# Causal scores from high and low float32r parts in a two-layer attention block on one Trainium2 core

## The chip, the cores and the metric

The kernel runs on one core of one Trainium2 chip. The metric is the device time of one execution in microseconds, the median of three runs. Four engines matter here: PE (TensorE, matmuls, with its weight loads shown apart as PEld), DVE (VectorE), ACT (ScalarE) and POOL (GpSimd). SP issues most DMAs from one queue, in order.

## The reference

The inputs are `x` and a context `y`, 16 batches of 256 tokens by 256 features, all float32. Three attentions follow one another for every batch, each with 16 heads of 16 features, and then an MLP:

```
layer 0:  x = rmsnorm(x + softmax(q k^T / 4) v Wo)      q from rmsnorm(x), k and v from rmsnorm(y)
layer 1:  h = ln(x);  q, k, v = h W + b;  rope(q), rope(k)
          s = where(tril, q k^T / 4, -inf);  x = x + softmax(s) v Wo      (causal)
layer 2:  h = ln(x);  q = h W, k and v = y W;  rope(q), rope(k)
          x = x + softmax(q k^T / 4) v Wo
mlp:      x = x + gelu(ln(x) W1 + b1) W2 + b2            (256 -> 1024 -> 256)
```

The code numbers the layers 0, 1 and 2. The "second layer" of the change is layer 1, the only causal one.

## The kernel before, in words

There are 48 attentions, 16 batches by three layers. The string `ORDER` sets the layer of each of the 48, so that layer 1 of a batch follows some attentions after its layer 0. An `Att` object holds one attention; its methods are its steps. Most methods are generators: each `yield` ends a piece that is emitted by itself.

The order of all pieces is written out by hand in the text `PLAN`. Each word names a step (`scores.18.0` is the first block of scores of attention 18, `q.19` a piece of the queries of attention 19), and each time a word stands there the next piece of its generator is emitted. The engines run their own instructions in the order in which they were emitted, so `PLAN` sets the order on PE, DVE, ACT, POOL and SP. The last attention's end and the MLPs (eight groups of two batches) come after `PLAN`.

The steps that the text below speaks of, with their lines:

- `q` (785) and `k` (840) make queries and keys by feature: 16 matmuls through `by_feature` (631), then for layers 1 and 2 the bias on ACT (758), the rope on DVE (766 swap, 772 two products, 808 or 861 or 864 the sum). `v` and `project` are 16 matmuls each through `by_token` (643).
- Attentions that are not fast: the queries are written twice into the tile `qm`, even rows kept in one copy and odd rows in the other (DVE 814, ACT 816). One 32-row group of PE then holds two heads.
- Fast attentions: `q_high` (821) rounds the queries to float32r on ACT, into both halves of the tile; `q_low` (828, 832) takes the rest on DVE and copies it; `q_out` (838) moves rows by two DMAs so that each row pair holds high and low parts. `k_high` (873, ACT), `k_low` (877, DVE) and `k_out` (885, two DMAs) do it for the keys, through the tile `hl`, of which there is one buffer. `qm` and `kT` have two each.
- `scores` (933) makes one block of scores into two PSUM tiles `S` of two banks each, the pool's only two, then exponentiates them on ACT (974, one instruction for each tile, into `pt`), and for layer 1 clears the upper triangle on POOL (982).
- `values` (1005) multiplies with the values into `A`; `take` and `take_last` (1020) copy that out; `heads_in`, `sums_in`, `invert` and `divide` normalise, by way of DMAs.

A block of scores in both forms, where `m` is the number of query columns:

```
if not self.fast:
    for half in range(2):
        ...
        for r, ps in rows:
            nc.tensor.matmul(ps[64 * half : 64 * half + 64, 2 * m * u : 2 * m * (u + 1)] ...,
                lhsT=self.kT[r, t, at], rhs=self.qm[r, t, :, q0:S], ...)
    continue
for i in range(2):
    for h in range(2):
        for r, ps in rows:
            nc.tensor.matmul(ps[:, at : at + m],
                lhsT=self.kd[r, i, t, kc * P : (kc + 1) * P].bitcast(F32R),
                rhs=self.qd[r, i, h, t, q0:S].bitcast(F32R), start=(h == 0), stop=(h == 1), ...)
```

`rows` are four row groups. Layers 0 and 2 have four blocks of one unit each, with `m` = 256. Layer 1 has three blocks: the first and the third are one unit with `m` = 256, the second is two units with `m` = 128 (the keys of the second half, which only the second half of the queries sees). Attentions 0 and 1 are never fast.

Of the kernel before, what the change touches and what calls it, by code (L numbers as in the profile page):

```python
# [30 lines left out]
FAST = (0, 2)  # L31
# [23 lines left out]
scores.0.0 q.1 scores.0.0 scores.0.0 v.0 spread.1 scores.0.1 spread.1 q.1 v.0 v.1 v.1 scores.0.1  # L55
v.0 load_piece.5.0 scores.0.1 v.1 stats_x.2 scores.0.2 stats_x.2 stats_x.3 values.0.0 scores.0.2
values.0.1 send.2 stats_x.3 scores.0.2 load_piece.5.3 send.3 values.0.1 scores.0.3 k.1 scores.0.3
send.2 scores.0.3 load_piece.5.2 k.2 send.3 k.1
scores.1.0 k_high.2 load_early.3 k_low.2 values.0.2 scores.1.0 stats_y.2 receive.2 q.2 scores.1.0
stats_y.2 scores.1.1 load_piece.5.1 values.0.3 scores.1.1 q.3 k_out.2 take_last.0 scores.1.1 q.2  # L60
scores.1.2 q_high.2 heads_in.0 values.1.0 q_low.2 scores.1.2 load_early.4 q_low.2 v.2 v.2
scores.1.2 stats_y.3 q_out.2 scores.1.3 v.2 values.1.1 receive.3 scores.1.3 stats_x.6 load.4 k.3
scores.1.3 values.1.1
scores.2.0 k_high.3 q.3 values.1.2 stats_y.3 scores.2.0 k_low.3 values.1.3 scores.2.0 heads_in.0
load_piece.6.0 take_last.1 q_high.3 load_early.0 scores.2.1 values.2.0 q_low.3 scores.2.1 k_out.3
k.4 q_low.3 scores.2.1 sums_in.0 stats_x.4 values.2.1 stats_x.4 scores.2.2 q_out.3 load_piece.6.3
send.4 v.3 scores.2.2 v.3 send.4 load_piece.6.2 scores.2.2 invert.0 v.3 k_high.4 divide.0
scores.2.3 stats_y.6 invert.0 values.2.1 q.4 scores.2.3 k_low.4 load_piece.6.1 sums_in.1
scores.2.3 values.2.2 receive.4
scores.3.0 invert.0 values.2.3 scores.3.0 heads_in.1 fold_of_att take_last.2 scores.3.0 q.4  # L70
heads_in.1 invert.1 scores.3.1 q_high.4 divide.0 invert.1 divide.1 values.3.0 k_out.4 scores.3.1
q_low.4 project.0 stats_y.4 scores.3.1 invert.1 q_low.4 stats_y.4 fold_of_att values.3.1 project.0
q_out.4 scores.3.2 stats_x.6 project.0 scores.3.2 send.6 project.0 stats_y.8 scores.3.2 finish.0
fold_of_att values.3.1 stats.5 scores.3.3 v.4 v.4 load_later.0 scores.3.3 divide.1 stats.5
scores.3.3 k.6 load_piece.7.0 norm.5 heads_in.2 v.4 load_piece.7.1
scores.4.0 load_early.1 k_high.6 values.3.2 scores.4.0 k_low.6 values.3.3 fold_of_att fold_of_att
scores.4.0 turn.5 take_last.3 sums_in.2 stats_y.6 scores.4.1 turn.5 q.5 scores.4.1 sums_in.3
stats_x.8 load_piece.7.3 scores.4.1 fold_of_att k_out.6 k.5 invert.2 q.5 stats_x.8 invert.2
scores.4.2 q.5 k.5 divide.2 values.4.0 q.5 scores.4.2 send.6 q.5 values.4.1 scores.4.2 heads_in.2
q.5 project.1 load_later.1 k.5 invert.2 k.5 v.5 k.5 project.1 heads_in.3 values.4.1 scores.4.3 q.5  # L80
q.5 receive.6 values.4.2 k.5 heads_in.3 scores.4.3 q.6 project.1 scores.4.3 invert.3 load_early.2
project.1 divide.2 values.4.3 invert.3 q.6 v.5 load_piece.7.2
scores.5.0 take_last.4 q_high.6 finish.1 v.6 v.6 sums_in.4 scores.5.0 q_low.6 scores.5.0 q_low.6
scores.5.0 stats.7 scores.5.0 scores.5.1 invert.3 v.6 stats.7 send.8 v.5 scores.5.1 q_out.6 norm.7
project.2 scores.5.1 pieces.7 send.8 scores.5.1 stats_y.10 scores.5.2 scores.5.1 heads_in.4
values.5.0 project.2 scores.5.2 pieces.7 receive.8 project.2 values.5.1 scores.5.2 k.8 heads_in.4
divide.3 divide.3 scores.5.2 values.5.1 invert.4 scores.5.2
scores.6.0 k_high.8 divide.4 project.2 pieces_in.7 values.5.2 scores.6.0 k_low.8 load_later.7
finish.2 project.3 scores.6.0 invert.4 take_last.5 stats.9 scores.6.1 project.3 stats.9 values.6.0
sums_in.5 scores.6.1 project.3 v.7 v.7 keep.5 scores.6.1 norm.9 invert.4 load_later.8 q.7 pieces.9  # L90
invert.5 pieces.9 v.7 divide.5 scores.6.2 invert.5 q.7 load_later.9 values.6.1 scores.6.2
heads_in.5 divide.4 k.7 q.7 scores.6.2 heads_in.5 q.7 values.6.1 q.7 scores.6.3 stats_y.8
pieces_in.9 k.7 q.7 values.6.2 scores.6.3 k.7 q.8 invert.5 scores.6.3 load_later.5 k.7 k.7 k_out.8
values.6.3 k.7 project.3 q.7 q.7 take_last.6 load_later.4
scores.7.0 divide.5 sums_in.6 q.8 project.4 scores.7.0 stats_x.10 scores.7.0 stats_x.10 project.4
q_high.8 scores.7.1 heads_in.6 scores.7.0 send.10 project.4 scores.7.0 project.5 send.10
scores.7.1 stats_y.10 q_low.8 heads_in.6 scores.7.1 q_low.8 scores.7.1 v.8 project.5 stats.11
scores.7.1 q_out.8 scores.7.2 finish.3 receive.10 v.8 stats.11 values.7.0 scores.7.2 invert.6
values.7.1 norm.11 invert.6 divide.6 scores.7.2 q.9 scores.7.2 pieces.11 values.7.1 v.8 scores.7.2
scores.8.0 keep.7 pieces.11 values.7.2 scores.8.0 load_later.6 k.10 invert.6 scores.8.0  # L100
load_later.3 take_last.7 load_piece.8.1 q.9 sums_in.7 scores.8.1 load_piece.8.2 k_high.10 q.9
values.8.0 load_piece.8.0 scores.8.1 q.9 k.9 load_later.10 k_low.10 scores.8.1 divide.6 heads_in.7
q.9 scores.8.2 k.9 q.9 values.8.1 scores.8.2 k.9 v.9 v.9 scores.8.2 k.9 heads_in.7 k.9 values.8.1
scores.8.3 pieces_in.11 q.9 q.9 values.8.2 k.9 scores.8.3 k.11 invert.7 stats_x.14 k_out.10
scores.8.3 divide.7 gain_ca
scores.9.0 v.9 k.11 invert.7 k.11 values.8.3 scores.9.0 k.11 q.10 scores.9.0 take_last.8
scores.9.0 k.11 invert.7 scores.9.0 scores.9.1 q.10 project.4 k.11 sums_in.8 q_high.10 values.9.0
finish.4 project.6 scores.9.1 q_low.10 scores.9.1 q_low.10 scores.9.1 v.10 divide.7 k_high.11
q_out.10 scores.9.1 k_low.11 heads_in.8 scores.9.2 v.10 keep.9 heads_in.8 invert.8 values.9.1
scores.9.2 project.6 q.11 invert.8 project.6 scores.9.2 scores.9.2 k_out.11 v.10 values.9.1  # L110
scores.9.2
scores.10.0 stats.13 q.11 values.9.2 scores.10.0 stats.13 q.11 project.7 scores.10.0 divide.8
norm.13 load_later.2 take_last.9 q.11 scores.10.1 heads_in.9 q.11 values.10.0 scores.10.1
project.7 invert.8 k.12 load_piece.9.0 q.11 scores.10.1 sums_in.9 pieces.13 load_piece.9.1
q_high.11 scores.10.2 stats.12 values.10.1 q_low.11 pieces.13 scores.10.2 stats.12 q_low.11
scores.10.2 norm.12 q_out.11 divide.8 k.12 turn.12 invert.9 values.10.1 scores.10.3 k.12 invert.9
turn.12 values.10.2 k.12 scores.10.3 heads_in.9 k.12 v.11 v.11 divide.9 scores.10.3 load_piece.9.2
k.12 pieces_in.13 stats.16 stats_x.14 k_high.12 q.12 k_low.12 load_piece.8.3 invert.9 v.11
values.10.3 q.12
scores.11.0 take_last.10 fold_of_fc1 stats.16 q.12 scores.11.0 project.8 q.12 scores.11.0 q.12  # L120
project.6 fold_of_fc1 norm.16 scores.11.1 heads_in.10 q.12 values.11.0 scores.11.1 send.14
project.8 send.14 k.13 scores.11.1 fold_of_fc1 q_high.12 k_out.12 scores.11.2 divide.9 values.11.1
q_low.12 scores.11.2 v.12 v.12 q_low.12 scores.11.2 pieces.16 q_out.12 values.11.1 stats_y.14
scores.11.3 k.13 load_piece.9.3 v.12 pieces.16 project.9 scores.11.3 stats_y.14 k.13 scores.11.3
k.13 keep.11 k.14 project.9 heads_in.11 stats.15 sums_in.10
scores.12.0 k.13 k_high.14 stats.15 values.11.2 k.13 scores.12.0 k_low.14 scores.12.0 norm.15
pieces.15 scores.12.1 finish.6 q.13 scores.12.1 project.8 pieces.15 fold_of_fc1 scores.12.1
receive.14 values.11.3 heads_in.10 q.13 invert.10 scores.12.2 take_last.11 divide.10 scores.12.2
q.13 heads_in.11 values.12.0 q.13 scores.12.2 values.12.1 q.13 sums_in.11 q.13 scores.12.3
values.12.1 gain_fc1.0 q.13 invert.10 values.12.2 q.13 pieces_in.15 scores.12.3 fold_of_fc1 q.14  # L130
scores.12.3 invert.11 stats_x.17
scores.13.0 divide.11 keep.12 q.14 k.15 scores.13.0 stats_x.17 invert.10 q_high.14 load_piece.10.0
v.13 scores.13.0 v.13 q_low.14 invert.11 scores.13.0 k.15 q_low.14 scores.13.0 scores.13.1
# [213 lines left out]
def xattn_kernel(  # L347
# [303 lines left out]
    def fast(i):  # L651

        return 1 < i < N_ATT and ORDER[i] in FAST

# [1408 lines left out]
```

## Time and profile before

| what | value |
| --- | --- |
| median of 3 runs (lowest to highest) | 910.98 us (907.81 to 911.55) |
| the profiled execution: its time, its span | 906.3 us, 904.5 us |
| busy share of the span: PE, PEld, DVE, ACT, POOL | 97%, 63%, 77%, 63%, 39% |
| attentions: first to last exponential | 12.0 to 697.5 us |
| granted PE clock, mean | 0.997 |
| instructions of the program in the trace | 32853 |

A float32 matmul stands in the trace as two records, a float32r matmul as one. A line of the timeline gives start, duration, engine, line, operation, output and inputs, shapes and the number of records; the time from one group's start to the next group's start is what the group took of PE. Busy time of PE is not PE at its peak, since the ends of matmuls are modelled.

### The profile page before, as it was taken

The numbers are of one execution on the slowest core, as the hardware profiler recorded it, in microseconds if no ns is written. First come the engines' busy times: TensorE is split into PE (matmuls) and PEld (weight loads), VectorE is DVE, ScalarE is ACT, GpSimd is POOL, SyncE is SP. The second block draws the span as 40 slices with busy tenths as digits, with TensorE's granted clock in tenths as the row PEclk, the third lists the DMA queues.
The fourth block names the chain that finished last, engine by engine and source line by source line (L and its number), as shares of the span: only waits on it lengthen the run. The fifth ranks groups of instructions, "written<-read, shape, count | busy, mean of one in ns | idle before, by whom it ended". The sixth has DMA issues, their size and how long they took to land.

```text
span 904.5 us, 32853 instructions
## 1 busy us (share of the span) xinstructions
PE 881.5 (97%) x13762; PEld 565.6 (63%) x13762; DVE 699.5 (77%) x1534; ACT 570.8 (63%) x801; POOL 352.3 (39%) x558
## 2 busy tenths in 40 slices
PE   8989999899999999999999999999999999999997
PEld 4455545555555555554555555555555799999997
DVE  5357978888888899779887889998885687777653
ACT  3776657676777767757766677776876633334440
POOL 3334664538172546265453353573132131111000
PEclk9999999999999999999999999999999999999999
DMA  8564445535343434452434332232432021112201
GB/s 280 199 201 144 150 143 174 166 115 168 117 157 125 140 109 143 145 173 85 137 118 147 100 123 83 87 115 97 148 112 74 25 68 60 57 35 65 71 25 50
DMA packets 101454, 107.04 MB, mean 118 GB/s; under 512 B 26602, under 2 KB 81778, under 8 KB 101298
## 3 DMA queue, kind: packets, MB, share of 16 engines
q1 hardware_dynamic: 96210, 89.89, 30.1%
q0 software_dynamic: 4400, 14.42, 5.4%
q8 instruction: 110, 1.80, 0.8%
q10 hardware_dynamic: 688, 0.54, 0.2%
q14 instruction: 46, 0.38, 0.1%
HBM read 46.33 MB, written 13.65 MB: 66 GB/s over the span
## 4 chain that ended last, share of the span: by engine, by line
PE 76%; DVE 9%; DMA 5%; ACT 3%; issue 3%; SPq 3%; POOL 1%; ACTq 0%; DVEq 0%; POOLq 0%
PE d L643 14%; PE d L631 14%; PE A L1005 13%; PE S L962 7%; PE upX L1219 6%; PE A L1317 6%; PE S L951 5%; PE downZ L1317 3%; PE upZ L1219 3%; ACT pt L974 2%; PE d L1317 2%; PE d L1219 2%; DVE u L772 1%; DMA turn_hop<-bits 1%; SPq L596 1%
## 5 line engine op out<-in xcount | busy, mean ns | idle before, releaser
L974 ACT ACTIVATE pt<-S 128x1024 f32<-128x1024 f32 x224 | 217.6, 1022 | 73.1 <-PE S L951 41.6
L1005 PE MATMUL A<-pt,va 128*32 128x256 f32 (+1 forms) x3072 | 186.8, 366 | 5.1 <-DVE av L1020 2.8
L974 ACT ACTIVATE pt<-S,sy 128x1024 f32<-128x1024 f32 x128 | 135.9, 1114 | 37.3 <-PE S L962 28.3
L1005 PEld LDWEIGHTS A<-pt,va 128*32 128x32 f32 x3072 | 87.0, 109 | 81.8 <-issue 16.7
L982 POOL TENSOR_SCALAR_AFFINE_SELECT pt<-pt 128x512 f32<-128x512 f32 x128 | 93.4, 750 | 66.5 <-ACT pt L974 65.8
L962 PEld LDWEIGHTS S<-qm,kT 32*128 32x128 f32 x1920 | 68.6, 183 | 56.9 <-issue 29.7
L962 PE MATMUL S<-qm,kT 32*128 32x256 f32 x1920 | 96.4, 304 | 6.1 <-ACT pt L974 4.7
L619 POOL TENSOR_TENSOR cur<-cur,bias 128x512 f32<-128x512 f32 x48 | 65.5, 1368 | 36.5 <-DVE xn L551 36.4
L758 ACT ACTIVATE a<-d,qk_bias 128x256 f32<-128x256 f32 x128 | 53.9, 475 | 31.2 <-PE d L631 25.8
L523 POOL TENSOR_SCALAR r_ln<-bmv 128x2 f32<-128x2 f32 x48 | 14.9, 311 | 143.2 <-DVE bmv L542 142.5
L951 PE MATMUL S<-qm,kT 32*64 32x512 f32 (+1 forms) x1152 | 67.6, 512 | 1.4 <-ACT pt L974 1.2
L631 PE MATMUL d<-hT,sa 128*32 128x256 f32 x1024 | 61.6, 380 | 0.1
L1241 ACT COPY g<-upX 128x512 f32<-128x512 f32 x28 | 15.0, 589 | 72.4 <-issue 68.1
L1063 POOL TENSOR_TENSOR seen<-seen,sums 128x64 f32<-128x64 f32 x48 | 17.1, 355 | 103.9 <-DVE sums L1049 102.2
L551 DVE TENSOR_SCALAR xn<-cur,bmv,r_ln 128x256 f32<-128x256 f32 x96 | 49.9, 568 | 5.3 <-POOL r_ln L524 5.3
L772 DVE TENSOR_TENSOR u<-u,turn 128x512 f32<-128x512 f32 x64 | 53.2, 831 | 0.0
L772 DVE TENSOR_TENSOR a<-a,turn 128x512 f32<-128x512 f32 x64 | 47.5, 742 | 1.8
L1257 ACT ACTIVATE g<-g,fb 128x256 f32<-128x256 f32 x96 | 41.0, 499 | 11.1 <-DVE g L1246 11.1
L766 DVE STREAM_SHUFFLE u<-a 128x512 f32<-128x512 f32 x64 | 47.8, 747 | 0.1
L1065 DVE TENSOR_TENSOR oT<-oT,inv 128x512 f32<-128x512 f32 x48 | 34.9, 728 | 15.7 <-DMA inv<-inv_hop 5.9
L631 PEld LDWEIGHTS d<-hT,sa 128*32 128x32 f32 x1024 | 32.8, 110 | 22.6 <-ACT hT L573 0.8
L1020 DVE COPY av<-A 128x512 f32<-128x512 f32 x47 | 32.2, 685 | 13.4 <-PE A L1005 13.1
(176 smaller groups left out, 1711.4 us busy)
## 6 DMA issues: line engine op xcount, KB each, us to landing
kT<-hl SPq DMA_DIRECT2D x60, 256.0 KB
qm<-qm SPq DMA_DIRECT2D x60, 256.0 KB
oT<-av SPq DMA_DIRECT2D x192, 64.0 KB
inv<-inv_hop SPq DMA_DIRECT2D x96, 128.0 KB
turn_hop<-bits SPq DMA_DIRECT2D x33, 256.0 KB
hT<-turn_hop SPq DMA_DIRECT2D x92, 64.0 KB
out<-res SPq DMA_DIRECT2D x15, 256.0 KB
cur<-in_x POOLq DMA_DIRECT2D x11, 256.0 KB, 3.7
```

The lines of the kernel that those rows point to most:

```text
L619: nc.gpsimd.tensor_tensor(t, t, bias_sb[:, row : row + D].unsqueeze(1).to_broadcast([P, NC, D]), ALU.add)
L631: nc.tensor.matmul(o, lhsT=w[:, k, at + t * P + j : at + t * P + j + 32], rhs=tokens, start=(k == 0), stop=(k == KC - 1), skip_group_check ...
L643: nc.tensor.matmul(ps[j : j + 32, c * D : (c + 1) * D], lhsT=some_tokens(src, k, c, j), rhs=w[:, k, at : at + D], start=(k == 0), stop=(k ...
L758: nc.scalar.activation(a[:, t], ps[:, t], AF.Identity, bias=bias[:, t : t + 1])
L772: nc.vector.tensor_tensor(t, t, table.unsqueeze(1).to_broadcast([P, KC, S]), ALU.mult)
L951: nc.tensor.matmul(ps[64 * half : 64 * half + 64, 2 * m * u : 2 * m * (u + 1)] .rearrange("p (i s) -> p i s", i=2), lhsT=self.kT[r, t, at] ...
L962: nc.tensor.matmul(ps[:, at : at + m], lhsT=self.kd[r, i, t, kc * P : (kc + 1) * P].bitcast(F32R), rhs=self.qd[r, i, h, t, q0:S].bitcast(F ...
L974: nc.scalar.activation(pt[:, :, :w], ps[:, :, :w], AF.Exp, scale=scale)
L982: nc.gpsimd.affine_select(out=diag, in_=diag, compare_op=ALU.is_ge, fill=0.0, base=0, pattern=[[0, 2], [0, 2], [1, P]], channel_multiplier=-1,
L1005: nc.tensor.matmul(self.av[32 * r : 32 * r + 32, i, q0:S], lhsT=self.va[:, kc, 8 * t + 2 * r + i, :], rhs=pts[r // 2][:, r % 2, i * m : (i ...
L1219: nc.tensor.matmul(o if len(b.shape) == 2 else by_groups(o), lhsT=a[:, c * P : (c + 1) * P], rhs=b, start=(first and c % 2 == 0), stop=Tru ...
L1317: nc.tensor.matmul(ps[:, c, :], lhsT=a[f // 2][:, f % 2, c * P : (c + 1) * P], rhs=b[:, f, :], start=(first and c == 0 and f == 0), stop=True,
```

## The change

`FAST` takes layer 1 in. The scores of the 16 causal attentions are then made by the float32r branch above: 16 matmuls of 128 by 256 for each of the two wide blocks, and 32 matmuls of 128 by 128 for the block with two units. Their `q` ends before the two masked copies (lines 814 and 816 are not reached any more in these 16), their `k` writes into `hl`, and they get the steps `q_high`, `q_low` (two pieces), `q_out`, `k_high`, `k_low` and `k_out`.

`PLAN` is written anew from its first words on. It has 2720 words for 2640: each causal attention has two pieces of `q` fewer and seven pieces of the new steps more; every other word stands there as often as before. The lines below `PLAN` move down by 11 in the changed kernel (962 becomes 973). Nothing else differs.

```diff
-FAST = (0, 2)
+FAST = (0, 1, 2)
...
 PLAN = """
...
-scores.18.0 heads_in.16 q.19 k.20 scores.18.0 q.19 heads_in.16 divide.15 scores.18.0 q.19
-invert.16 k_high.20 scores.18.1 q.19 k_low.20 project.15 scores.18.1 take_last.17 stats.23
-scores.18.1 sums_in.17 divide.16 stats.23 scores.18.2 project.15 values.18.0 scores.18.2 norm.23
...
+scores.18.0 q.19 k_high.20 divide.16 load_piece.11.0 values.17.2 invert.16 scores.18.0 k_low.20
+values.17.3 q.19 scores.18.0 k_out.20 q.19 k.19 take_last.17 scores.18.1 divide.15 values.18.0
+heads_in.16 scores.18.1 q.19 project.15 scores.18.1 k.19 sums_in.17 k.19 q_high.19 scores.18.2
+k.19 receive.20 heads_in.16 values.18.1 q_low.19 scores.18.2 q_low.19 v.19 scores.18.2 k.19
+q_out.19 invert.17 k_high.19 scores.18.3 k_low.19 values.18.1 q.20 scores.18.3 stats_x.24 k_out.19
...
```

## The prediction

> **What bounds the kernel now.** I read the busy shares first, then busy time by stage, the waits, the timeline of PE, and the groups by shape. First two lines of the page, then an answer for the stretch in which only attentions run (columns: length, then busy time and instructions of PE, PEld, DVE, ACT and POOL, granted clock, DMA share and GB/s):
>
> ```profile
> PE 881.5 (97%) x13762; PEld 565.6 (63%) x13762; DVE 699.5 (77%) x1534; ACT 570.8 (63%) x801; POOL 352.3 (39%) x558
> PE 76%; DVE 9%; DMA 5%; ACT 3%; issue 3%; SPq 3%; POOL 1%; ACTq 0%; DVEq 0%; POOLq 0%
> 12.00:686.60 674.60, 660.25 (x12096) 370.05 (x12100) 553.72 (x1211) 480.13 (x611) 317.02 (x500) 1.00 0.43 138
> ```
>
> PE is busy 98% of the attention stage and holds three quarters of the chain of waits, so a microsecond less of matmul is nearly a microsecond less of time, as long as DVE (82% here) lets it. The MLPs, after 697 us, are not touched.
>
> The timeline of PE gives what a block of scores costs. Each line has the start, the duration, the engine and the line first.
>
> ```profile
> 308.91 1.93 PE L1005 MATMUL A<-pt,va 128*32 128x256 f32 x32
> 310.66 1.91 PE L631 MATMUL d<-hT,sa 128*32 128x256 f32 x32
> 312.50 0.74 PE L962 MATMUL S<-qm,kT 32*128 32x256 f32 x16
> 313.17 1.07 PE L1005 MATMUL A<-pt,va 128*32 128x256 f32 x16
> ...
> 318.49 1.11 PE L951 MATMUL S<-qm,kT 32*64 32x512 f32 x16
> 319.53 1.93 PE L643 MATMUL d<-cao,oT 128*32 128x256 f32 x32
> 321.28 1.91 PE L643 MATMUL d<-ca,yT 128*32 128x256 f32 x32
> 323.12 1.12 PE L951 MATMUL S<-qm,kT 32*64 32x256 f32 x32
> 324.17 1.93 PE L631 MATMUL d<-hT,sa 128*32 128x256 f32 x32
> ```
>
> From start to next start, the float32r block takes 313.17 - 312.50 = 0.67 us. The float32 block takes 1.04 us when it is one wide unit (318.49 to 319.53) and 1.05 when it is two narrow ones (323.12 to 324.17); I use 1.04 for both.
>
> Third, the groups on DVE and ACT that the change removes or multiplies, and two weight loads:
>
> ```profile
> L828 DVE TENSOR_TENSOR qm<-a,qm 128x512 fp32r<-128x512 f32 x16 | 13.1, 819 | 3.8 <-ACT qm L821 3.7
> L832 DVE CAST qm<-qm 128x512 fp32r<-128x512 f32 x30 | 13.5, 450 | 1.0
> L877 DVE TENSOR_TENSOR hl<-hl 128x512 fp32r<-128x512 f32 x16 | 11.6, 726 | 1.4 <-ACT hl L873 1.2
> L814 DVE TENSOR_SCALAR qm<-a,vec 128x512 f32<-128x512 f32 x16 | 7.8, 484 | 0.5
> L821 ACT CAST qm<-a 128x1024 fp32r<-128x1024 f32 x16 | 16.8, 1048 | 12.4 <-DVE a L808 7.2 <-issue 4.5 <-ACT hT L573 0.7
> L873 ACT CAST hl<-hl 128x512 fp32r<-128x512 f32 x16 | 10.0, 626 | 1.1 <-DVE hl L861 0.5 <-ACT av L1020 0.5
> L816 ACT ACTIVATE qm<-a,vec 128x512 f32<-128x512 f32 x16 | 11.6, 725 | 7.6 <-DVE a L808 6.6 <-ACT pt L974 0.9
> ...
> L962 PEld LDWEIGHTS S<-qm,kT 32*128 32x128 f32 x1920 | 68.6, 183 | 56.9 <-issue 29.7 <-ACT pt L974 19.3 <-ACT av L1020 4.3
> L1005 PEld LDWEIGHTS A<-pt,va 128*32 128x32 f32 x3072 | 87.0, 109 | 81.8 <-issue 16.7 <-POOL pt L982 13.2 <-ACT av L1020 1.8
> ```
>
> **PE, the wide blocks.** Layer 1 has two a causal attention, of a shape that layers 0 and 2 run already: 2 x (1.04 - 0.67) = 0.74 us saved.
>
> **PE, the narrow block.** 32 float32r matmuls of 128 columns against 128 weight columns have no row in the trace. The block of 0.67 us is four waves, each one matmul in each of the four row groups. A float32 record is two passes, and 16 records of `values` in four column groups take 0.89 us for 256 columns and 0.46 for 128 (medians of the timeline), so passes scale with columns; the 32 records of a dense product, 16 passes of 256 one after another in each column group, take 1.72 at the least, 0.107 a pass. Four waves are 0.43, and 0.24 is left for filling and draining. The narrow block is eight waves:
> - streaming alone, 0.053 a wave: 8 x 0.053 + 0.24 = 0.67;
> - float32 speed, four passes, 0.213 a wave: 8 x 0.213 + 0.24 = 1.95;
> - bound by weight loads: a load of 32 columns lasts 109 ns and one of 128 lasts 183, so a column costs (183 - 109) / 96 = 0.77 ns and 128 columns some 99 ns; with the wave's own overhead 0.107, hence 8 x 0.107 + 0.24 = 1.10.
>
> I take 1.10. The float32r records are single and 256 columns run at one pass, and the load's row is of the same weight shape. The ends stay for the range. So the narrow block does not gain: 1.04 becomes 1.10.
>
> The Trainium skill, TensorE: Matmul & The Clock Gate, section "LDWEIGHTS (loading the stationary operand)", states a load time of columns / 1.2 ns, which is 107 ns for 128 and agrees with the rows above; it speaks against this half of the change. The same page's "Back-to-back issue gap" has N / 2.4 + 2.5 ns for a matmul, 56 ns for 128 columns; by that rule alone the block would be an estimated 8 x 0.056 + 0.24 = 0.69 us and the whole saving 6.6 us larger.
>
> Sum on PE: 16 x (0.74 - 0.06) = **-10.9 us** (bounds: 16 x (0.74 + 0.37) = -17.8 and 16 x (0.74 - 0.91) = +2.7).
>
> **DVE.** Per causal attention: plus 0.82 (828), 0.45 (832), 0.73 (877), minus 0.48 (814), and the keys' sum into `hl` 0.77 for 0.74: +1.55, x16 = +24.7 us. Hidden only where PE has more to do. I cut `PLAN` into 47 stretches, from the first piece of `scores.i.0` to that of `scores.(i+1).0`, and added the durations of the pieces in each: 1.78 for 16 dense matmuls, 0.67 or 1.04 a block of scores, 0.87 for `values` (0.43 narrow), and DVE and ACT rows by their mean. Against the trace the totals need a factor: PE 622.6 x 1.033 = 643 (a dense group mostly takes 1.84), DVE 591.5 by words where the trace is busy 553.7 (means overlap a little; 0.925 fits the middle of the stage). With these, the larger engine of each stretch adds up to 649.6 before, and the trace took 674.5 from the first exponential of attention 0 to that of attention 47. So this sum misses 25 us of smaller waits. DVE exceeds PE by 6.4 us in all before, and by 10.9 after: worst in the stretches of attentions 18 and 37 (13.7 PE, 15.7 DVE each), 10 (12.9, 14.6), 4 and 20 (1.3 each). That is **+4.5 us** given back. Behind a late `q_low` on DVE stand `q_out` on SP and everything SP has behind it: `invert`, `k_out`, `heads_in`, whose landings `divide` and then `project` await.
>
> **ACT.** +1.05 + 0.63 - 0.73 = 0.95 a causal attention, 15 us in all, on an engine busy 71% of the stage; no stretch has ACT above PE by this. Cost nothing, hidden under PE; without that cover 15 us.
>
> **The spacing of score blocks.** The two `S` tiles come free after two exponentials (2 x 1.02, and some 0.2 to start), so less than 2.25 us of other matmuls between two blocks makes PE wait. Summed over the 176 blocks, that shortfall is 20.8 us in the old order and 14.0 in the new: layer 0 loses most of it (8.0 to 2.5). Stretch by stretch the trace's stalls go with it only in part (a correlation of 0.65), so half counts: **-3.4 us** (0 to -6.8).
>
> **New DMAs.** 64 issues more on SP, at 0.60 us (median of `k_out`'s issues) 38 us on a queue that is far from full, and 16.8 MB on engines 43% busy. They must land before `scores.i.0`. The chain shows 3.25 us for one landing of `kT` and 3.66 and 2.40 for `qm`. In the new order, PE work between `k_out` or `q_out` and the scores is at least 3.6 us in 31 of the 32 causal cases; `k_out.19` has only 1.9. I allow **+2 us** for that and for the single `hl` buffer, now used by every attention (0 to +6).
>
> **Sum:** -10.9 + 4.5 - 3.4 + 2 = -7.8 us. The profiled execution took 906.3 us (span 904.5 and 1.8 around it) and would take 898.5; the median of the runs is 4.7 above it, so 911.0 - 7.8 = **903 us**. Anything within 0.5% (4.6 us) can't be told from no change.
>
> **Rivals.**
> - *Narrow matmuls stream freely* (0.67 a block): 6.9 us more, 896. For it: 128 columns halve exactly in `values`. Against: those loads have only 32 columns.
> - *Narrow matmuls run at float32 speed* (1.95): -7.8 + 16 x 0.85 = +5.8, 917. For it: no float32r row under 256 columns. Against: the mode belongs to the operand, and 256 columns run at one pass. It decides from about 1.6 us a block.
> - *DVE becomes the bound* (the slower side): if each DVE piece holds its engine for its full mean, the larger engine of the stretches adds up to 649.4 before and 655.8 after, +6.4, with nothing back for spacing: 917. It decides, by this sum, once DVE exceeds PE by some 19 us over the stretches instead of 10.9 (10.9 + 7.8): then nothing of the gain is left. For it: 12 of the 47 stretches come out with DVE at PE's level or above. Against: before, stretches such as attention 5 (10.1 PE, 11.5 DVE) took 10.2 us, since DVE runs ahead into its neighbours.
> - *The change doesn't do what it says*, two records a matmul as in float32: excluded, since 1920 matmuls of the same form have one record each.
>
> **Chances.** Forecast 0.55, free streaming 0.15, float32 speed 0.13, DVE 0.17. Faster by over 0.5%: three quarters of the forecast and all of free streaming, 0.56. Same: 0.23. Slower: 0.21, the most part of the two slow rivals and a little of the forecast. The range 893 to 919 leaves out the tail of free streaming with full spacing gain and that of both slow rivals together.
>
> **What would show it.** Right: wide causal blocks at 0.67 from start to start, narrow ones near 1.10 with waves 0.107 apart, DVE busy some 20 us more in the stage, ACT 15 us more, no long wait of the causal scores for `kT` or `qm`. Wrong: narrow blocks over 1.6 us; PE waiting on dense products for DVE's `hT` or `oT`; PE's busy share of the stage below 95%.

## The result, and the profile after

| | before | after |
| --- | --- | --- |
| median (20 runs each) | 911.17 us | 902.21 us |
| lowest to highest | 906.73 to 916.83 | 897.72 to 909.80 |
| profiled execution, span | 906.3, 904.5 us | 904.37, 902.6 us |
| granted PE clock of the profiled execution | 0.997 | 0.989 |

The ratio is 0.9901, with a 95% interval of 0.9879 to 0.9923: about 9 us faster, where 7.8 was forecast. The profiled execution of the changed kernel is one of its longer ones, so its span is not to be set against that of before; the busy times are.

First the engines' busy shares and the chain's shares on the page of the changed kernel, then the attention stage, from the first exponential of attention 0 to that of attention 47:

```profile
PE 868.3 (96%) x13762; PEld 580.2 (64%) x13762; DVE 715.6 (79%) x1566; ACT 583.8 (65%) x817; POOL 356.7 (40%) x558
PE 60%; DVE 15%; DMA 9%; SPq 4%; issue 4%; ACT 4%; POOL 3%; ACTq 0%; DVEq 0%; POOLq 0%
...
11.50:684.30 672.80, 647.57 (x12096) 384.98 (x12100) 567.86 (x1244) 493.16 (x627) 321.58 (x501) 0.99 0.51 164
```

PE lost 13.2 us of busy time, DVE gained 16.1 and ACT 13.0. PE still fills 96% of the stage (647.57 of 672.80), but its part of the chain fell from 76% to 60% (66% in a second profile of the same kernel, `after_again` below): DVE, DMA and SP's queue took the rest. The kernel is nearer to having several bounds at once.

The blocks of scores on the timeline of PE in the changed kernel, where line 962 has become 973:

```profile
150.43 1.05 PE L1016 MATMUL A<-pt,va 128*32 128x256 f32 x16
151.41 1.11 PE L973 MATMUL S<-qm,kT 32*128 32x128 f32 x32
152.45 1.07 PE L1016 MATMUL A<-pt,va 128*32 128x256 f32 x16
...
160.75 0.75 PE L973 MATMUL S<-qm,kT 32*128 32x256 f32 x16
161.43 1.07 PE L484 MATMUL d<-fc,vec 128*32 128x256 f32 x16
```

A wide block takes 161.43 - 160.75 = 0.68 us from start to start. The narrow one, which no row of before showed, takes 152.45 - 151.41 = 1.04, against 1.05 as float32. So the whole saving in the scores' PE time comes from the 32 wide blocks.

The groups on DVE that grew, after:

```profile
L888 DVE TENSOR_TENSOR hl<-hl 128x512 fp32r<-128x512 f32 x32 | 24.1, 752 | 1.2 <-ACT hl L884 1.1
L839 DVE TENSOR_TENSOR qm<-a,qm 128x512 fp32r<-128x512 f32 x32 | 22.6, 708 | 3.4 <-ACT qm L832 3.4
L843 DVE CAST qm<-qm 128x512 fp32r<-128x512 f32 x46 | 22.2, 482 | 0.9
```

And what PE waited for (total in us, times, longest):

```profile
PE d L654 <- DVE oT L1076: 7.8, 7, 2.0
PE S L973 <- ACT pt L985: 4.2, 12, 0.6
PE S L973 <- DMA qm<-qm: 3.4, 5, 1.3
PE d L642 <- DVE va L928: 2.4, 1, 2.4
PE A L1016 <- DVE av L1031: 2.1, 2, 1.1
...
PE d L642 <- DMA hT<-turn_hop: 2.0, 3, 1.0
```

The first, the third and the last line are new: before, PE never waited for the divided heads (`oT`) or for a landing of `qm` or `hT`. They are small. The first is not the scores' doing: `order_alone`, below, has it too. The third is, but only two of its five waits stand before causal scores (attentions 9 and 13, 1.2 us together); the other three stand before attentions 14 and 37, of layers 0 and 2.

### The profile page after: what moved, and what is told of

It is laid out like the page before. It is cut to its first block, busy times and chain, and to the rows that moved or that the text cites. A ratio compares the mean times of both kernels' runs of the same rounds, so it can differ in the third digit from the quotient of the medians.

```text
span 902.6 us, 33008 instructions
## 1 busy us (share of the span) xinstructions
PE 868.3 (96%) x13762; PEld 580.2 (64%) x13762; DVE 715.6 (79%) x1566; ACT 583.8 (65%) x817; POOL 356.7 (40%) x558
## 4 chain that ended last, share of the span: by engine, by line
PE 60%; DVE 15%; DMA 9%; SPq 4%; issue 4%; ACT 4%; POOL 3%; ACTq 0%; DVEq 0%; POOLq 0%
PE d L654 11%; PE d L642 10%; PE A L1016 9%; PE S L973 7%; PE upX L1230 6%; PE A L1328 6%; DMA inv<-inv_hop 3%; PE downZ L1328 3%; PE upZ L1230 3%; ACT pt L985 3%; DMA qm<-qm 2%; PE d L1328 2%; DVE u L783 2%; PE d L1230 2%; DVE xn L562 1%
## 5 line engine op out<-in xcount | busy, mean ns | idle before, releaser
L973 PEld LDWEIGHTS S<-qm,kT 32*128 32x128 f32 x2944 | 101.2, 184 | 79.0 <-issue 45.0
L973 PE MATMUL S<-qm,kT 32*128 32x256 f32 (+1 forms) x2944 | 138.2, 300 | 8.2 <-ACT pt L985 4.2
L1016 PEld LDWEIGHTS A<-pt,va 128*32 128x32 f32 x3072 | 94.9, 111 | 63.3 <-issue 7.0
L993 POOL TENSOR_SCALAR_AFFINE_SELECT pt<-pt 128x512 f32<-128x512 f32 x128 | 96.8, 778 | 50.7 <-ACT pt L985 50.3
L1074 POOL TENSOR_TENSOR seen<-seen,sums 128x64 f32<-128x64 f32 x48 | 20.0, 417 | 109.6 <-DVE sums L1060 109.4
L1076 DVE TENSOR_TENSOR oT<-oT,inv 128x512 f32<-128x512 f32 x48 | 35.4, 737 | 18.9 <-DMA inv<-inv_hop 13.2
L1323 DVE TENSOR_TENSOR g<-g,g 128x512 f32<-128x512 f32 x64 | 40.5, 681 | 0.0
L832 ACT CAST qm<-a 128x1024 fp32r<-128x1024 f32 x32 | 33.6, 1049 | 9.8 <-issue 4.1
```

Source lines behind the costliest of these rows:

```text
L973: nc.tensor.matmul(ps[:, at : at + m], lhsT=self.kd[r, i, t, kc * P : (kc + 1) * P].bitcast(F32R), rhs=self.qd[r, i, h, t, q0:S].bitcast(F ...
L993: nc.gpsimd.affine_select(out=diag, in_=diag, compare_op=ALU.is_ge, fill=0.0, base=0, pattern=[[0, 2], [0, 2], [1, P]], channel_multiplier=-1,
L1016: nc.tensor.matmul(self.av[32 * r : 32 * r + 32, i, q0:S], lhsT=self.va[:, kc, 8 * t + 2 * r + i, :], rhs=pts[r // 2][:, r % 2, i * m : (i ...
```

## The experiments

The theory: PE gains about 0.37 us in each of 32 wide blocks, 11.8 us, and nothing in the narrow ones; some of it is given back through DVE's added work and landings, and the new order adds a little. Rivals: the gain is the new order's alone; DVE has become the bound; or the new DMAs are what gives back. The kernels ran on different chips, and each ratio is to the kernel before on the same chip. Differences between two ratios are worked out as if their errors were independent. Of the variants, only `dve_relief`, `parts_twice` and `filled_wait` stand on a chip on which the changed kernel is known to have run (`after_again`). For the others its ratio of 0.990 is carried over from chip to chip, which no run checks.

### What is the order's, and what the scores'

`order_alone`:

```diff
-FAST = (0, 1, 2)
+FAST = (0, 2)
 PLAN: k_high, k_low, k_out, q_out and the second q_low of causal attentions left out,
       their q_high and first q_low replaced by q
```

> The new order of the steps with the causal scores as they were, in float32; the steps of the high and low parts are left out, and the two masked copies of the queries come back in the places of q_high and the first q_low. Theory (the gain is PE time of the causal blocks, 0.37 us for each of 32 wide blocks and nothing for the narrow ones, 11.8 us, with some 4 given back through DVE and landings): most of the gain is gone, 907 to 913 us. Rival (the gain is the new order's spacing of the score blocks): 899 to 904 us, no slower than the changed kernel's 902.2.

Measured: 903.36 us against 906.75, ratio 0.9966 (0.9944 to 0.9987). `after_again`, the changed kernel beside two others further down:

> The changed kernel itself, unaltered, beside the other three, so that they have it on the same chip. The recorded ratio is 0.990 to the kernel before, and all theories expect 0.988 to 0.992 here.

Measured: 899.31 against 908.16, ratio 0.9898 (0.9870 to 0.9927). So the order alone brings 0.34%, 3.1 us, and the scores the rest: 0.9901 / 0.9966 is 0.9935, 6 us, with an error of about 3. Both theories were half right. By microseconds the run lies in the rival's range, but that range was stated for another chip; the ratios put about a third of the gain on the order and two thirds on the scores.

The groups of score matmuls show the same two parts. In `order_alone`:

```profile
L936 PE MATMUL S<-qm,kT 32*128 32x256 f32 x1920 | 95.5, 306 | 3.4 <-ACT pt L948 3.3
L925 PE MATMUL S<-qm,kT 32*64 32x512 f32 x640 | 45.2, 613 | 0.0
L925 PE MATMUL S<-qm,kT 32*64 32x256 f32 x512 | 18.2, 387 | 0.0
```

In the changed kernel:

```profile
L973 PE MATMUL S<-qm,kT 32*128 32x256 f32 x2432 | 120.1, 304 | 8.2 <-ACT pt L985 4.2 <-DMA qm<-qm 3.4 <-issue 0.5
L973 PE MATMUL S<-qm,kT 32*128 32x128 f32 x512 | 18.1, 277 | 0.0
L962 PE MATMUL S<-qm,kT 32*64 32x512 f32 x128 | 8.9, 612 | 0.1
```

`order_alone` sums to 158.9 us of busy time and the changed kernel to 147.1: 11.8 less, the forecast's price of the wide blocks. The kernel before had 96.4 + 49.0 + 18.7 = 164.1:

```profile
L962 PE MATMUL S<-qm,kT 32*128 32x256 f32 x1920 | 96.4, 304 | 6.1 <-ACT pt L974 4.7 <-issue 0.5
L951 PE MATMUL S<-qm,kT 32*64 32x512 f32 x640 | 49.0, 612 | 1.4 <-ACT pt L974 1.2
L951 PE MATMUL S<-qm,kT 32*64 32x256 f32 x512 | 18.7, 387 | 0.0
```

The order took 5.2 us of it, with the same matmuls, and in the trace fewer blocks sit half done: nine of the 40 wide causal blocks lasted over 1.3 us from first to last matmul before, two in `order_alone`.

The two profiled executions also show what the 11.8 us became. First the stage in `order_alone` (the changed kernel's stands above) and its wait for the divided heads, then a group of 32 records in the changed kernel at half the granted clock, where others take 1.93 us:

```profile
11.50:684.00 672.50, 654.24 (x12118) 368.64 (x12116) 548.10 (x1212) 481.41 (x612) 317.70 (x500) 0.99 0.43 139
PE d L617 <- DVE oT L1039: 7.7, 5, 2.7
...
313.89 3.64 PE L642 MATMUL d<-yT,ca 128*32 128x256 f32 x32 [2.40 <-DVE va L928]
```

Between the two PE's busy time in the stage fell by 654.24 - 647.57 = 6.7 us only. The changed kernel's profile has 17.1 us of its stage at half clock and `order_alone`'s 6.8; half of the difference is 5.1 us, which makes up the 11.8. PE's idle time rose by 7.0 us, from 18.3 to 25.2, and so the stage took equally long in both. Of that rise 5.4 us are waits for landings of `qm` (3.4) and `hT` (2.0), which `order_alone` does not have. The wait for the divided heads is no part of it, 7.7 us against 7.8: it came with the new order. The profile of the changed kernel has a low clock, 0.989; over its runs the mean is 0.993, against 0.994 in `order_alone`, so in a typical run the clock's part is an estimated 1 us.

### What a microsecond of PE is worth, and what bounds the narrow block

`narrow_f32`:

```diff
+dt = F32R if m == S else F32
-lhsT=self.kd[...].bitcast(F32R), rhs=self.qd[...].bitcast(F32R),
+lhsT=self.kd[...].bitcast(dt), rhs=self.qd[...].bitcast(dt),
```

> The changed kernel with the narrow causal block (128 by 128) multiplied as float32 instead of float32r, on the same tiles; 32 matmuls, all else the same. Its PE time should go from 1.04 us in the changed kernel's timeline to about 1.95, 16 times, +14.6 us. Theory (PE sets the time of the attention stage one to one): 913 to 918 us, and the forecast's price of that rival is confirmed. Rival (DVE has become the bound and PE has room): less than half of it, below 909 us.

Measured: 912.29 against 906.75, ratio 1.0056 (1.0033 to 1.0078). The block on its timeline:

```profile
211.34 2.07 PE L974 MATMUL S<-qm,kT 32*128 32x128 f32 x64
213.33 0.85 PE L654 MATMUL d<-w,yT 128*32 128x256 f32 x12
...
L974 PE MATMUL S<-qm,kT 32*128 32x128 f32 x1024 | 33.5, 277 | 0.0
```

It takes 213.33 - 211.34 = 1.99 us from start to start, as 14 of the 16 do to within 0.01 us (two take 2.17 and 2.28). The group is busy for 33.5 us where the changed kernel's is for 18.1, so there are 15.4 us more on PE. The time rose by 1.0056 - 0.9901 = 1.55%, 14 us, with an error of 3. So about nine tenths of added PE time reach the end, PE sets most of the time still, and the rival that DVE has become the bound (under half) falls. This is the worth of PE time that is added; of the PE time that the change took away, about half arrived.

`narrow_64m`:

```diff
+n = m if m == S else m // 2
+for o in range(0, m, n):
     ... ps[:, at + o : at + o + n], rhs=self.qd[r, i, h, t, q0 + o : q0 + o + n]
```

> The changed kernel with each matmul of the narrow causal block cut in two of 64 moving columns, with the same 128 weight columns loaded twice as often. Theory (a wave lasts as long as its weight load, 0.111 us in the changed kernel's trace): 16 waves for 8, the block goes from 1.04 to about 1.93 us, and waves stay 0.11 apart. Rival (a wave lasts as long as its moving columns need plus a share): the block stays near 1.04, waves 0.06 apart.

One run, with a profile:

```profile
210.56 1.98 PE L975 MATMUL S<-qm,kT 32*128 32x64 f32 x64
212.47 0.85 PE L654 MATMUL d<-w,yT 128*32 128x256 f32 x12
```

The block takes 212.47 - 210.56 = 1.91 us (again 14 of the 16; two take 2.09 and 2.19). Its single records start in waves of four, and after the first wave, which takes longer, the waves are 0.112 us apart for 64 moving columns. In the changed kernel those of 128 moving columns are 0.111 apart, and those of 256 are 0.118 (medians). So a wave of 64 moving columns costs as much as one of 128. That is the theory's side, and the weight loads of the narrow block start in waves 0.11 apart too. No run has this form with fewer weight columns, so that it is the load of 128 columns, and not some other fixed time of a wave, fits the sizes but is not shown by itself. The narrow block has eight waves where a wide one has four, and so it gains nothing over float32.

### Is DVE's added work what gives back?

Of 11.8 us saved on PE, 6 arrive, with an error of 3. `dve_relief` leaves out work on DVE of about the size that was added:

```diff
-self.times(u, sin_t)
+if not self.causal:
+    self.times(u, sin_t)
```

> The changed kernel without the product of the swapped queries and keys with the sine table in the causal attentions (one piece of q and one of k, 0.83 us each on DVE), which the scores then lack: 26.6 us less on DVE, about what the change added (24.7). All else stays. Theory (part of the 11.8 us saved on PE is given back because DVE has 24.7 us more to do): 3 to 7 us faster than the changed kernel. Rival (DVE's added work is hidden; what is given back is landings and the clock): within 2 us of it.

Measured: 895.17 against 908.16, ratio 0.9867 (0.9832 to 0.9903), beside `after_again` at 0.9898. The medians differ by 4.1 us and the ratios by 0.3%, on the theory's side; but the difference has an error of about 0.45%, so it is not shown.

`low_on_act`:

```diff
-nc.vector.tensor_copy(self.qd[:, 1, 1]..., self.qd[:, 0, 1])
+copy = nc.scalar.copy if self.causal else nc.vector.tensor_copy
+copy(self.qd[:, 1, 1]..., self.qd[:, 0, 1])
```

> The changed kernel with the copy of the queries' low parts (second piece of q_low, 0.45 us on DVE) made by ACT for the causal attentions: 7.2 us less on DVE, about 10 us more on ACT. Theory (DVE's work gives back some 4.5 us in the stretches where it exceeds PE): 1 to 4 us faster, 898 to 901 us. Rival (what is given back is waiting for landings and the half clock that follows, not DVE): 901 to 904 us, no change; slower if ACT's order, where exponentials wait behind the copy, matters more.

Measured: 898.94 against 906.75, ratio 0.9912 (0.9882 to 0.9942): no difference from the changed kernel that can be told, but the error is 3 us, and the theory asked for 1 to 4. `low_on_pool`:

```diff
 k_low, and q_low's second piece:
+eng = nc.gpsimd if self.causal else nc.vector
```

> The changed kernel with the causal attentions' k_low and the second piece of q_low on POOL instead of DVE: 18.9 us less on DVE, some 35 us more on POOL (its sums of 128x512 take 1.37 us). Theory (DVE's added work gives back 3 to 4 us, as the run without the sine products showed): 1 to 3 us faster than the changed kernel, ratio 0.986 to 0.989. Rival (POOL's in-order queue, which clears triangles and takes roots, delays the parts or these steps): no faster, 0.990 or above.

Measured: 905.41 against 907.03, ratio 0.9968 (0.9941 to 0.9996): slower than the changed kernel by some 6 us, if the ratio of 0.990 holds on this chip. PE's wait for the divided heads is 9.9 us in its profile:

```profile
PE d L654 <- DVE oT L1078: 9.9, 7, 4.5
PE S L975 <- DMA qm<-qm: 4.2, 4, 1.4
```

The changed kernel's two profiles have 7.8 and 9.0 us there, and 3.4 and 3.7 for `qm`, so neither line explains 6 us. That POOL, which runs its own steps in order, brings the parts later is likely and not shown. Moving DVE's work to another busy engine gained nothing that could be measured in either run.

### Are the new DMAs what gives back?

`parts_on_pool`:

```diff
-nc.sync.dma_start(out=rows[1 - i : P : 2], in_=rows[i:P:2])          # q_out, and k_out likewise
+(nc.gpsimd if self.causal else nc.sync).dma_start(...)
```

> The changed kernel with the 64 DMAs of the causal high and low parts (q_out and k_out) issued from POOL's queue instead of SP's: 38 us of issues less on SP, some 49 us more on POOL at 0.76 each. Theory of landings (the loads of the inverted sums and heads stand behind the new issues on SP, DVE waits for them, then PE for the divided heads): 2 to 5 us faster, 897 to 900 us, and DVE's wait for the inverted sums goes back from 13 us towards the 6 of the kernel before. Rival (DVE's own work, or the DMA engines' load): no change, 901 to 904 us; slower if POOL's in-order queue delays q_out behind the clearing of triangles.

Measured: 898.67 against 906.75, ratio 0.9915 (0.9888 to 0.9942): no change. DVE's wait for the inverted sums did fall as the theory of landings said. The changed kernel has the first line, this run the second:

```profile
DVE oT L1076 <- DMA inv<-inv_hop: 13.2, 8, 4.0
DVE oT L1076 <- DMA inv<-inv_hop: 5.2, 5, 2.3
```

The time did not follow. So the place of these DMAs in SP's queue costs no more than the error of 3 us. `parts_twice`:

```diff
+for _ in range(1 + self.causal):
     nc.sync.dma_start(...)                                          # q_out and k_out
```

> The changed kernel with each of the 64 DMAs of the causal high and low parts issued twice, the same bytes again: 64 issues (38 us) more on SP and 16.8 MB more, as much as the change added. Theory of landings (the change's own DMAs cost 2 to 5 us through SP's queue and the engines): 2 to 6 us slower than the changed kernel. Rival (they are hidden, only DVE's work gives back): within 2 us of it.

Measured: 1059.62 against 908.16, ratio 1.169 (1.1658 to 1.1722), far outside both. What SP waited for:

```profile
SPq L850 <- DMA qm<-qm: 77.3, 32, 4.1
SPq L898 <- DMA kT<-hl: 66.5, 32, 4.8
```

The second copy writes where the first does, so SP stood still for each landing, 64 times and 144 us in all, with everything behind it in the queue. The run failed as a test of load: it added a wait. It does show that such waits are not hidden: with the 64 added transfers they made the run 160 us longer than the changed kernel beside it. `parts_extra` adds as many bytes without that wait:

```diff
+t = dram.tile([P, 2 * S], F32, tag="more", bufs=16)
+nc.sync.dma_start(out=t, in_=turn_sb)                               # behind each of the 64
```

> The changed kernel with one more DMA of 256 KB from SP behind each of the 64 of the causal parts, from a constant tile to scratch memory that nothing reads: as many issues and bytes again as the change added, but with no wait for the landing of the same data. Theory of landings (the change's own DMAs cost PE time through SP's queue and the DMA engines): 2 to 6 us slower than the changed kernel, 0.992 to 0.997. Rival (hidden): within 2 us of it, 0.988 to 0.992.

Measured: 924.75 against 907.03, ratio 1.0184 (1.0142 to 1.0226). That is 2.8% above the changed kernel, 26 us, where at most 6 were expected. PE waits three times as long for `qm` and more for turned inputs:

```profile
PE d L654 <- DVE oT L1080: 10.9, 9, 2.7
PE S L977 <- DMA qm<-qm: 10.0, 12, 2.0
PE d L642 <- DMA hT<-turn_hop: 6.6, 3, 4.4
```

So 64 further DMAs are not hidden. Whether the change's own 64 cost as much can't be read from this: these go to memory and not within the chip, and they come on top of a busier machine.

### Do PE's waits before the projections cost what they seem to?

`late_project`:

```diff
 PLAN: the first piece of project.0, .1, .5, .8 and .17 moved one or two PE steps later, as in
-... project.0 q_low.3 scores.2.2 stats_y.6 q_low.3 heads_in.1 scores.2.2 values.2.1 project.0
+... q_low.3 scores.2.2 stats_y.6 q_low.3 heads_in.1 scores.2.2 values.2.1 project.0 project.0
```

> The changed kernel with the first piece of project.0, .1, .5, .8 and .17 one or two PE steps later in the order (past the next score or value product). In the traces of the changed kernel and of its variants PE waits in front of these five for the divided heads, 0.9 to 3.3 us each, some 7 to 9 us in all. Theory (these waits are real gaps on PE, and half-clock stretches of 3.4 us follow some of them): 4 to 9 us faster than the changed kernel's ratio of 0.990, so 0.980 to 0.986. Rival (the wait only moves: what stands behind them waits instead, or layer 1 of these batches starts later): within 2 us of it.

Measured: 904.34 against 907.03, ratio 0.9960 (0.9932 to 0.9989): slower than the changed kernel, if anything. The waits for divided heads are nearly gone from its profile, and others have come in their place:

```profile
PE S L944 <- ACT pt L956: 10.6, 16, 3.1
PE A L987 <- DVE av L1002: 2.6, 3, 1.1
PE d L548 <- DVE xn L533: 1.9, 1, 1.9
PE d L625 <- DVE oT L1047: 1.6, 4, 0.7
```

The first line stood at 4.2 us. The score blocks come in a row and wait for their exponentials: the wait moved, as the rival said. `filled_wait`:

```diff
 by_token, for project.0, .1, .5, .8, .17:
+for _ in range(idle):
+    nc.tensor.matmul(ps, lhsT=ident, rhs=w0_sb[:, 0, 0:512], ...)   # 9 in all, overwritten
```

> The changed kernel with one to three products of constant tiles (128x512 float32, 0.86 us each, nine in all) put on PE right ahead of project.0, .1, .5, .8 and .17, into the same PSUM tile, which the real product then overwrites: PE works through most of the time that it waits there in the changed kernel. Theory (PE's waits bring the half-clock stretches, and those cost 3 to 4 us of the median run): the mean granted clock rises from 0.993 to 0.995 or more, the stretches near 66 and 130 us go, and the time falls by 1 to 4 us, ratio 0.986 to 0.989. Rival (the stretches do not hang on these waits, or the products delay PE themselves): clock 0.993, no faster, 0.990 or above.

Measured: 899.43 against 907.47, ratio 0.9911 (0.9878 to 0.9945), no different from the changed kernel's 0.9898 on the same chip. The granted clock did rise: its mean over the runs is 0.9956, for 0.993 of the changed kernel, and in the profile one half-clock stretch of 3.4 us is left in the attentions where the changed kernel's had four, one of them twice as long. The time did not follow by an amount that could be measured. Over the 20 runs of the changed kernel a mean clock lower by 0.01 goes with 8 us more time (a correlation of -0.85), so a clock higher by 0.0025 should be worth an estimated 2 us, and the difference of the two ratios has an error of 4. Whether the half-clock stretches cost time of their own, or only mark the waits that cost it, stays open.

None of the variants beats the changed kernel beyond the intervals.

## Why the prediction was right, point by point

**Wide blocks, 0.74 us an attention.** Right: 0.68 from start to start where 0.67 was taken, and 11.8 us less busy time of score matmuls than with the same order and the old scores.

**Narrow block, 1.10 with bounds of 0.67 and 1.95.** Right in mechanism, a little high in size: 1.04. The waves are 0.111 apart where 0.107 was taken from loads of 32 and 128 columns (99 ns, and 8 of the wave's own, for which no row stood); filling and draining came to 1.04 - 8 x 0.111 = 0.15 where 0.24 was taken. The back-to-back rule of the Trainium skill (TensorE: Matmul & The Clock Gate, "Back-to-back issue gap"), taken alone, would have made it 0.69; the same section says that at few columns this rule counts too little, since it leaves out the weight load. Here a wave of 128 moving columns took 0.111 us where it has 0.056. The same page's rule on loads, 107 ns for 128 columns, is near the 0.111 and 0.112 measured, and `narrow_64m` speaks for it.

**DVE, +24.7 us of work and 4.5 of time.** The work was sized about right, and its effect on DVE's busy time was not. Added up by groups as the prediction did, it came to 26.7 us; DVE's busy time grew by 16.1 us, and by 20.2 from `order_alone` (695.4 to 715.6). DVE's instructions overlap in the trace, by 72 us in all before and 83 after; the prediction took a factor of 0.925 for that in its totals, but not in this term. The price of 4.5 is in line with the 4.1 between the medians of `dve_relief` and `after_again`, but not shown. Where the price would fall was wrong: the stretch of attention 18, with DVE put at 15.7, took 14.5 us, and that of attention 20 took 22.3, though DVE was busy for 19.2 of it: PE waited there 2.4 us for DVE and ran 6.8 us at half clock. A sum of stretches did not say where.

**Spacing of the blocks, -3.4 us.** In line with `order_alone`, 3.1 us for the whole new order, though that holds all its other effects too, among them 7.7 us of waits for the divided heads that the kernel before did not have.

**Landings, +2 us.** The mechanism is there: a new wait of PE for `qm`, 3.4 us in five places. Three of these are not before causal scores, where the prediction looked for them. The price is not settled; `parts_extra` says that further DMAs are much dearer here than the term allowed. That the queue is far from full did not settle what a DMA costs.

**Sum, -7.8 us.** 9.0 measured (0.9901 of 911.17). PE and the order brought more than forecast, 11.8 and 3.1 for 10.9 and 3.4, 14.9 in all for 14.3. What was given back is then 5.9 us, with an error of about 3, where 6.5 was forecast. That these two agree is in part luck: neither of the two terms behind the 6.5 is shown in its size, and the granted clock, a mean of 0.997 over the runs of the kernel before beside the variants and of 0.993 after, had no term.

**The rivals.** Free streaming is out, by the block of 1.04 and by `narrow_64m`. Float32 speed for the narrow block would have cost 1.55% (forecast: 13.6 us, measured 14), so its price was right and its condition false. DVE as the bound is out, since about nine tenths of added PE time arrive.

**What stays open:** how the 6 us that PE saved and the time did not get divide between DVE's work, the landings and the granted clock.

## What to carry to other kernels

Price a matmul form that the trace lacks by its waves: the larger of the moving columns and the weight load, plus filling and draining; halving the moving columns under a full weight load saved nothing here. When a schedule is rewritten along with a computation, run the new schedule with the old computation, because a third of a gain can be the schedule's. A wait that the profile puts before one product can be only where a later chain shows; moving or filling it gained no time here that could be measured.

## What the runs showed of the hardware

- Waves of four float32r matmuls in four row groups, with 128 weight columns each, start 0.112 us apart for 64 moving columns and 0.111 for 128 (0.118 for 256).
- A float32r matmul of 64, 128 or 256 moving columns stands in the trace as one record. The block of 32 matmuls of 128 by 128 takes 1.04 us in float32r and 2.00 in float32.
- The granted clock halves for 3.4 us or 6.8 us beside some waits of PE of 1 to 2.4 us in an otherwise busy stretch: four places in the attentions of the changed kernel's profile, one before. Others of the same size, such as one of 2.0 us that ended at 65.4 us, had no such stretch.
- 64 more DMAs of 256 KB, with the DMA engines half busy in the stage (a share of 0.51), cost 26 us. 64 that repeated a DMA just issued to the same place made SP wait 144 us for landings, and the kernel took 160 us longer.
